# An FP4 feed-forward's weights: turned by TensorE from raw tiles, or loaded in 32 by 32 blocks and turned in place by VectorE

## The chip, the cores and the metric

The kernel runs on one core of a Trainium2 chip. The metric is the device time of one execution in microseconds (us), and the median of several runs is compared. A profile of one execution gives the time of every instruction on the engines: TensorE (PE, with its weight loads as PEld), VectorE (DVE), ScalarE (ACT), GpSimd (POOL) and SyncE (SP), whose queue issues nearly all DMA transfers.

## The reference, cut to what matters

One transformer layer in float32 over x of 8 sequences, 1,024 tokens, 512 features: a latent attention block with 16 heads (causal softmax, clipped scores, rotary part), then a feed-forward block whose matrices and activations are quantized to FP4 (E2M1) in blocks of 16 along the contracted dimension.

```
def fp4_quant_dequant(x):            # blocks of 16 along the last dim
    scale = max(max|x| of the block / 6, 1e-12)
    return nearest value of (0, .5, 1, 1.5, 2, 3, 4, 6) to |x / scale| * sign * scale

def fp4_linear(x, w):                # w is (n, k)
    return einsum('bsk,nk->bsn', fp4_quant_dequant(x), fp4_quant_dequant(w))

x = x + attention(layernorm(x))
x = x + fp4_linear(silu(fp4_linear(y, w_gate)) * fp4_linear(y, w_up), w_down)   # y = layernorm(x)
```

w_gate and w_up are 1408 by 512, w_down is 512 by 1408. They are quantized along their rows, but the matmuls contract over those rows' elements, so the kernel needs them turned: the contracted dimension on the partitions.

## The kernel before, in words

The work is cut into 16 units of 512 tokens (two per sequence). `attention(u)` runs over four groups of four heads, and in each over the key blocks: 3 score steps per group in the even units (12 in all), 7 in the odd ones (28), which also see the first half of their sequence. A score step (`score_step`) has TensorE write scores of four heads into the one PSUM score tile `sc_ps`; ScalarE takes the exponential into a tile `pT` (a ring of three, which the output projection's `wo` shares); the clamp that stands for the clip is done for one half by VectorE (L645) and for the other by GpSimd (L648); on the diagonal GpSimd masks (L653). TensorE then multiplies by the values (`num`), one score step late (`flush(1)`), so that the next scores stand ahead of it in its order. In even units VectorE sums the probabilities (L680), in the first odd ones TensorE does (`den`). At the end of a group VectorE turns and inverts the sums (L737 to L740).

Between score steps the function pops *fillers*: pieces of the next unit's projections (loading x, L375; norms; from unit 4 on, and for unit 2, VectorE turns x in blocks and 16 DMAs per 256 tokens, L410, move the blocks into `xnT`), and in units 0 to 3 the pieces of the weight preparation. From unit 4 on the fillers are the feed-forward of earlier units. The output projection of unit u-1 (`po`, four tiles, 14 us of TensorE) runs in unit u behind the DMA of `wo` (L795), with VectorE adding the residual (L814) and SP storing it (`mid`).

TensorE, VectorE, ScalarE and GpSimd execute in the order in which the program writes their instructions. The SP queue's order is chosen by the scheduler of the language, which puts transfers that wait for nothing early. SP keeps eight semaphores for its DMAs; a transfer waits for the one eight before it.

A small planner (`Clock`) keeps estimated times of the engines. VectorE work without a fixed place is put into two queues by `slack`, and laid into estimated gaps (`fill`). `need(key)` lays everything up to the last entry of that key at once.

The weights: `weight_pieces` cuts w_gate and w_up into 11 chunks of 128 rows, w_down into 4. `load(i)` fetches a chunk into raw tiles of 128 rows by up to 512 columns (L310, rows of 2 KB) and queues `quantize` on them: per part a block maximum (L226), six short scale instructions for the whole step (L242 to L247), then per part six passes (L266, L274, L277, twice L280, L262). A `piece` then needs that chunk, has TensorE turn it in 128 by 128 squares (`turn`, L208) into a PSUM bank of the shared ring of three, and ScalarE copies the bank into the final tile `wg_T`, `wu_T` or `wd_T` (L210). The same `quantize` serves the activations, which are kept turned already: there, with `turned=True`, VectorE's block transpose (L236) is laid before the maximum and after the last pass.

How many weight pieces each of the first four units takes is written out by hand:

```
if u < FIRST:
    upto = n_weights * (5, 16, 23, 37)[u] // 37
```

Of the kernel before, what the change touches and what calls it, by code (L numbers as in the profile page):

```python
# [11 lines left out]
F32 = mybir.dt.float32  # L12
# [6 lines left out]
P = 128  # L19
# [8 lines left out]
NDC = D // P  # L28
NFC = FF // P
BLK = 16  # L30
FCH = [(0, 512), (512, 512), (1024, 384)]
# [11 lines left out]
def tile_mla_then_fp4_ffn(  # L43
# [17 lines left out]
    nc = tc.nc  # L61
# [5 lines left out]
    ring = ctx.enter_context(tc.tile_pool(name="ring", bufs=9))  # L67
# [12 lines left out]
    class Clock:  # L80


        pe = dve = act = silu = 0.0
# [27 lines left out]
    clk = Clock()  # L111
# [91 lines left out]
    def turn(src, dst, n):  # L203

        pt = bank("pt").rearrange("p (n k) -> p n k", k=P)
        tile_shape("whole")
        for i in range(n):
            nc.tensor.transpose(pt[:, i, :], src[:, i * P : (i + 1) * P], ident)  # L208
            clk.pe += 0.11
        on_act(0.56, lambda: nc.scalar.copy(dst, pt[:, 0:n, :]))  # L210


    def quantize(parts, key, turned=False, ready=0.0):

        ends, at = [], 0
        for part in parts:
            ends.append((at, at + part.shape[1] // BLK))
            at = ends[-1][1]
        nb = at
        got = {}  # L220

        def amax(k):
            if k == 0:
                got["sc"] = p1.tile([P, 88], F32, tag="sc", name="sc")[:, :nb]
                got["rs"] = p1.tile([P, 88], F32, tag="rs", name="rs")[:, :nb]
            nc.vector.tensor_reduce(  # L226
                got["rs"][:, slice(*ends[k])],
                parts[k].rearrange("p (b k) -> p b k", k=BLK),
                AX.X,
                ALU.max,  # L230
                apply_absolute_value=True,
            )

        def turn_blocks(part):
            slack(
                0.06 + 0.0013 * part.shape[1], lambda: nc.vector.transpose(part, part), key  # L236
            )

        def scales():
            sc, rs = got["sc"], got["rs"]  # L240

            nc.vector.tensor_scalar(sc, rs, 1.0 / 6.0, None, ALU.mult)  # L242
            nc.vector.scalar_tensor_tensor(rs, sc, -4.0, rs, ALU.mult, ALU.add)
            nc.vector.scalar_tensor_tensor(rs, sc, -2.0, rs, ALU.mult, ALU.add)
            nc.vector.scalar_tensor_tensor(sc, rs, 1.0 / 6.0, sc, ALU.mult, ALU.add)
            nc.vector.tensor_scalar(sc, sc, 1e-12, None, ALU.max)
            nc.vector.reciprocal(rs, sc)  # L247

        for k, part in enumerate(parts):
            if turned:  # L250
                turn_blocks(part)
            slack(0.06 + 0.0012 * part.shape[1], lambda k=k: amax(k), key, ready=ready)
        slack(1.1 + 0.008 * nb, scales, key)
        for part, end in zip(parts, ends):
            step, bl = part.shape[1], slice(*end)
            nbl = step // BLK
            part3 = part.rearrange("p (b k) -> p b k", k=BLK)

            def times(which, part3=part3, bl=bl, nbl=nbl):
                by = got[which][:, bl].unsqueeze(2).to_broadcast([P, nbl, BLK])  # L260
                if which == "sc":
                    nc.vector.tensor_tensor(part3, part3, by, ALU.mult)  # L262
                else:


                    nc.vector.scalar_tensor_tensor(  # L266
                        part3, part3, BELOW_ONE, by, ALU.mult, ALU.mult
                    )

            def steps(part=part, step=step):
                got["m"] = m = p1.tile([P, 512], F32, tag="m", name="m")[:, :step]
                nc.vector.tensor_scalar(  # L274
                    m.bitcast(U32), part.bitcast(U32), EXP_MASK, None, ALU.bitwise_and
                )
                nc.vector.tensor_scalar(m, m, 1.0, MAGIC, ALU.max, ALU.mult)  # L277

            def to_grid(op, part=part):
                nc.vector.tensor_tensor(part, part, got["m"], op)  # L280

            pass_cost = 0.06 + 0.00125 * step
            slack(pass_cost, lambda f=times: f("rs"), key)
            slack(1.2 * pass_cost, steps, key)
            slack(pass_cost, lambda f=to_grid: f(ALU.add), key)
            slack(pass_cost, lambda f=to_grid: f(ALU.subtract), key)
            slack(pass_cost, lambda f=times: f("sc"), key)
            if turned:
                turn_blocks(part)


    def weight_pieces():

        chunks = []
        for c in range(NFC):
            rows = slice(c * P, (c + 1) * P)
            chunks.append([(w_gate[rows, :], wg_T[:, :, rows]), (w_up[rows, :], wu_T[:, :, rows])])
        for c in range(NDC):
            rows = slice(c * P, (c + 1) * P)
            chunks.append([(w_down[rows, :], wd_T[:, :, rows])])  # L300
        raws = {}

        def load(i):

            raws[i] = []
            for src, _ in chunks[i]:
                for off in range(0, src.shape[1], 512):
                    width = min(512, src.shape[1] - off)
                    raw = ring.tile([P, 512], F32, tag="h", name="wraw")[:, :width]
                    nc.sync.dma_start(out=raw, in_=src[:, off : off + width])  # L310
                    raws[i].append(raw)
            quantize(raws[i], ("w", i))

        def piece(i, k, dst, off, n):
            clk.need(("w", i))
            turn(raws[i][k], dst[:, off : off + n], n)
            if k == len(raws[i]) - 1:
                raws.pop(i)
                if i + 3 < len(chunks):
                    load(i + 3)  # L320

        pieces = []
        for i, parts in enumerate(chunks):
            if len(parts) > 1:
                pieces += [(i, k, dst, 0, NDC) for k, (_, dst) in enumerate(parts)]
            else:
                pieces += [
                    (i, k, parts[0][1], off // P, width // P) for k, (off, width) in enumerate(FCH)
                ]
        begun = [(0.5, lambda i=i: load(i)) for i in range(3)]  # L330
        return begun + [(0.5, lambda x=x: piece(*x)) for x in pieces]


    def normed(xt, key):
# [564 lines left out]
    def up(m, k):  # L899
        while silus:  # L900
            silus.popleft()()
        h = hs[m][k]
        pg = hidden(m, wu_T, k)
        on_dve(
            0.1 + 0.00115 * h.free_size(),
            max(clk.pe + 0.3, clk.silu),
            lambda: nc.vector.tensor_tensor(h, pg, h, ALU.mult),  # L907
        )
        for group in ((0, 1), (2, 3), (4,), (5,)) if m == pairs - 1 else ((0, 1), (2, 3), (4, 5)):
            if k == group[-1]:  # L910
                quantize([flat(hs[m][j]) for j in group], ("h", m, k // 2), True)
        if k == NS - 1:
            yTs.pop(m)

# [101 lines left out]
    for u in range(n_units):  # L1016
        if u > 0:
            urgent.extend(lambda t=t, aTs=aTs: out_proj(u - 1, t, aTs) for t in range(NT))
        own = []
        if u + 1 < n_units:  # L1020
            own.extend(project_pieces(u + 1))
            content, rotary = quad_pieces(u + 1, 0)
            own.extend([(1.7, content), (0.9, rotary)])
        take = []
        if u < FIRST:
            upto = n_weights * (5, 16, 23, 37)[u] // 37
            while weight_work and n_weights - len(weight_work) < upto:
                take.append(weight_work.popleft())

            for _ in range(8 if u == FIRST - 1 else 0):  # L1030
                c, n, run = ffn.popleft()
                take.append((c, run, n))
        else:

            left = sum((13, 5)[v % 2 == 0] for v in range(u, n_units))
            within = sum(c for c, n, _ in ffn if n < len(tiles) - NT)
            budget = within * (13, 5)[u % 2 == 0] / left
            if u in (n_units - 3, n_units - 2):

                budget -= 40.0  # L1040
            while ffn and budget > 0 and ffn[0][1] < NT * u:
                c, n, run = ffn.popleft()
                budget -= c
                take.append((c, run, n))
        fillers.extend(merged(own, take))
        aTs = attention(u)
        while fillers:
            fillers.popleft()[1]()
# [88 lines left out]
```

## Time and profile before

| what | value |
|---|---|
| median of 3 runs | 3523.83 us (3519.83 to 3523.85) |
| the profiled execution | 3518.86 us, its span 3517.1 us |
| PE, DVE, ACT, POOL busy in the span | 98%, 83%, 38%, 22% |
| first and last transposing matmul on a raw weight tile | 67.6 and 424.0 us |
| raw weight tiles: transposing matmuls, ScalarE copies, loads | 132, 34, 34 |
| DMA traffic of the execution | 148.46 MB, 190,066 packets |

A line of the page or of an answer names the source line, the engine, the operation, the tiles (output, then inputs) and the shape; "128x512 f32 x30 | 23.6, 786" are 30 instructions, busy 23.6 us in sum, 786 ns each in the mean; a third number is the time for which the engine stood idle ahead of them, and behind an arrow what ended that. In a view by windows each engine has its busy time and its count of instructions in the stretch. The timeline gives start, length, engine, line and tiles.

### The profile page before, as it was taken

To read this page: it belongs to the slowest core of one execution; us is meant where nothing else is said; L and a number is where in the kernel's file an instruction comes from. 1 tells how busy PE (TensorE), PEld (TensorE's weight loads), DVE (VectorE), ACT (ScalarE), POOL (GpSimd) and SP (SyncE) were. 2 spreads that over 40 slices of the span, in tenths; PEclk is the share of its full clock that TensorE was granted. 3 is DMA by queue.
4 is the path that set the end of the run, shared out by engine and by line. 5 is a ranking of instruction groups with operands and counts; after the bars stand their busy time and mean duration, and the time that the engine had idled before them with its cause. 6 is when DMAs were issued, how large, how long until landed. Compare 5 with 4: busy or idle time off the path is not lost. (4 is left out here: it accounts for less than half of the span.)

```text
span 3517.1 us, 101866 instructions
## 1 busy us (share of the span) xinstructions
PE 3440.5 (98%) x45428; PEld 1526.8 (43%) x45428; DVE 2923.4 (83%) x5308; ACT 1326.2 (38%) x1850; POOL 769.0 (22%) x1086
## 2 busy tenths in 40 slices
PE   8999999999999999999999999999999999999999
PEld 3333344444444444444444444444444444444444
DVE  6878759789977889887989778899778988699887
ACT  4444443434333343333343333434343333333211
POOL 3333322112121221221221212212212222111100
PEclk9999999999999999999999999999999999999999
DMA  3212111111021101121110211111211111100110
GB/s 98 70 49 71 47 36 52 50 36 30 20 64 32 55 26 32 35 59 50 32 32 20 67 29 54 30 32 32 61 49 32 32 32 49 50 20 20 56 32 17
DMA packets 190066, 148.46 MB, mean 42 GB/s; under 512 B 126524, under 2 KB 128060, under 8 KB 189628
## 3 DMA queue, kind: packets, MB, share of 16 engines
q1 hardware_dynamic: 187780, 141.09, 13.5%
q8 instruction: 356, 5.83, 0.7%
q10 hardware_dynamic: 1848, 0.87, 0.1%
q14 instruction: 82, 0.67, 0.1%
HBM read 94.72 MB, written 33.55 MB: 36 GB/s over the span
## 5 line engine op out<-in xcount | busy, mean ns | idle before, releaser
L629 ACT ACTIVATE pT<-sc_ps 128x1024 f32<-128x1024 f32 (+1 forms) x640 | 566.3, 937 | 1069.4 <-PE sc_ps L122 835.8
L648 POOL TENSOR_SCALAR pT<-pT 128x1024 f32<-128x1024 f32 (+1 forms) x320 | 337.7, 1055 | 2325.4 <-ACT pT L629 2247.0
L122 PE MATMUL pg<-yT,wu_T 128*32 128x256 f32 x11264 | 638.5, 380 | 0.0
L122 PE MATMUL pg<-yT,wg_T 128*32 128x256 f32 x11264 | 634.5, 379 | 1.7 <-ACT yT L859 0.8
L122 PE MATMUL pd<-wd_T,h 128*32 128x512 f32 x5632 | 616.8, 592 | 2.9 <-DVE h L236 2.9
L122 PEld LDWEIGHTS pg<-yT,wg_T 128*32 128x32 f32 x11264 | 366.2, 110 | 276.9 <-issue 37.2
L680 DVE TENSOR_TENSOR pT<-pT 128x1024 f32<-128x1024 f32 (+3 forms) x528 | 459.8, 898 | 25.3 <-POOL pT L653 21.7
L122 PEld LDWEIGHTS pg<-yT,wu_T 128*32 128x32 f32 x11264 | 360.0, 110 | 264.6 <-issue 33.5
L645 DVE TENSOR_SCALAR pT<-pT 128x1024 f32<-128x1024 f32 (+1 forms) x320 | 229.3, 716 | 195.8 <-ACT pT L629 194.7
L122 PEld LDWEIGHTS pd<-wd_T,h 128*32 128x32 f32 x5632 | 182.3, 110 | 415.8 <-issue 389.8
L122 PE MATMUL sc_ps<-qc,kT 32*128 32x512 f32 (+3 forms) x3072 | 338.3, 525 | 10.8 <-ACT pT L629 10.8
L141 ACT COPY h<-pg 128x512 f32<-128x512 f32 x192 | 105.5, 550 | 629.6 <-PE pg L122 629.6
L122 PE MATMUL num<-pT,v 128*32 128x512 f32 (+3 forms) x3072 | 314.0, 496 | 17.4 <-POOL pT L653 16.9
L122 PE MATMUL sc_ps<-qr,kr 32*128 32x512 f32 (+3 forms) x3072 | 306.3, 483 | 6.9 <-DVE qr L564 6.7
L280 DVE TENSOR_TENSOR h<-h,m 128x512 f32<-128x512 f32 (+1 forms) x384 | 259.6, 676 | 10.1
L236 DVE STREAM_TRANSPOSE h<-h 128x512 f32<-128x512 f32 (+1 forms) x384 | 249.9, 658 | 4.9
L653 POOL TENSOR_SCALAR_AFFINE_SELECT pT<-pT 128x256 f32<-128x256 f32 (+1 forms) x384 | 231.3, 622 | 25.2 <-DVE pT L645 10.7
L122 PE MATMUL po<-wo,aT 128*32 128x512 f32 x2048 | 225.1, 596 | 9.1 <-DMA wo<-in_w_o_dram 4.5
L907 DVE TENSOR_TENSOR h<-pg,h 128x512 f32<-128x512 f32 x192 | 122.9, 640 | 118.5 <-PE pg L122 110.6
L122 PEld LDWEIGHTS sc_ps<-qc,kT 32*128 32x128 f32 x3072 | 114.3, 183 | 208.7 <-issue 149.8
L122 PEld LDWEIGHTS sc_ps<-qr,kr 32*128 32x128 f32 x3072 | 144.0, 185 | 114.1 <-issue 77.8
L122 PEld LDWEIGHTS num<-pT,v 128*32 128x32 f32 x3072 | 64.5, 108 | 220.8 <-issue 119.0
(97 smaller groups left out, 3528.5 us busy)
## 6 DMA issues: line engine op xcount, KB each, us to landing
xo<-in_x_dram SPq DMA_DIRECT2D x64, 256.0 KB, 2.7
wo<-in_w_o_dram SPq DMA_DIRECT2D x16, 1024.0 KB, 5.2
mid<-xo SPq DMA_DIRECT2D x64, 256.0 KB, 2.8
y<-mid SPq DMA_DIRECT2D x64, 256.0 KB, 2.8
xr<-mid SPq DMA_DIRECT2D x64, 256.0 KB, 2.7
out_dram<-xr SPq DMA_DIRECT2D x64, 256.0 KB, 2.0
xp<-in_x_dram SPq DMA_DIRECT2D x30, 512.0 KB, 3.8
xnT<-xp SPq DMA_DIRECT2D x416, 32.0 KB, 2.0
```

Of the source, the lines that this page charges most:

```text
L122: nc.tensor.matmul(dst, **kw)
L141: on_act(0.1 + 0.0009 * src.free_size(), lambda: nc.scalar.copy(dst, src))
L236: 0.06 + 0.0013 * part.shape[1], lambda: nc.vector.transpose(part, part), key
L280: nc.vector.tensor_tensor(part, part, got["m"], op)
L629: lambda: nc.scalar.activation(part, sc[:, 2 * k : 2 * k + 2, :cols], AF.Exp, scale=SM_SCALE),
L645: lambda: nc.vector.tensor_scalar(part, part, E_HI, E_LO, ALU.min, ALU.max),
L648: nc.gpsimd.tensor_scalar(part, part, E_HI, E_LO, ALU.min, ALU.max)
L653: nc.gpsimd.affine_select(out=diag, in_=diag, pattern=[[0, 2], [0, len(segs)], [1, P]], compare_op=ALU.is_ge, fill=0.0, base=0, channel_mu ...
L680: lambda a=whole, b=part: nc.vector.tensor_tensor(a, a, b, ALU.add),
L907: lambda: nc.vector.tensor_tensor(h, pg, h, ALU.mult),
```

## The change

Weights are no longer loaded as rows into raw tiles. Each part of the final tile (128 partitions, up to 512 columns) is loaded by four DMAs, one for each 32 partitions; a DMA takes blocks of 32 rows by 32 columns (pieces of 128 B) to where the turned block will stand. `quantize` runs in place on two such parts at a time. Behind the last pass, VectorE's block transpose turns each 32 by 32 block where it lies. The matmuls on the identity and the ScalarE copies go. There are 9 works (three column ranges of each of gate and up, three groups of chunks of w_down), 35 parts, 18 quantizing steps and 140 DMAs; with the two first loads and a last `need`, 21 pieces, divided over the units as 4, 10, 16, 21. A work is loaded two works ahead, and a step needs the one before it to be laid.

```diff
-    def quantize(parts, key, turned=False, ready=0.0):
+    def quantize(parts, key, before=False, after=False, ready=0.0):
...
         for k, part in enumerate(parts):
-            if turned:
+            if before:
                 turn_blocks(part)
...
-            if turned:
+            if after:
                 turn_blocks(part)
...
-        chunks = []
-        for c in range(NFC):
-            rows = slice(c * P, (c + 1) * P)
-            chunks.append([(w_gate[rows, :], wg_T[:, :, rows]), (w_up[rows, :], wu_T[:, :, rows])])
-        for c in range(NDC):
-            rows = slice(c * P, (c + 1) * P)
-            chunks.append([(w_down[rows, :], wd_T[:, :, rows])])
-        raws = {}
+        works = []
+        for off, width in FCH:
+            for w, dst in ((w_gate, wg_T), (w_up, wu_T)):
+                src = w[off : off + width, :].rearrange("(f a) (c q b) -> q c a f b", a=32, q=4, b=32)
+                parts = [dst[:, c, off : off + width] for c in range(NDC)]
+                works.append((src, parts))
+        src = w_down.rearrange("(f a) (c q b) -> q c a f b", a=32, q=4, b=32)
+        for c0, n in ((0, 4), (4, 4), (8, 3)):
+            cs = range(c0, c0 + n)
+            works.append((src[:, c0 : c0 + n], [wd_T[:, c, :] for c in cs]))
 
         def load(i):
-            raws[i] = []
-            for src, _ in chunks[i]:
-                for off in range(0, src.shape[1], 512):
-                    width = min(512, src.shape[1] - off)
-                    raw = ring.tile([P, 512], F32, tag="h", name="wraw")[:, :width]
-                    nc.sync.dma_start(out=raw, in_=src[:, off : off + width])
-                    raws[i].append(raw)
-            quantize(raws[i], ("w", i))
-
-        def piece(i, k, dst, off, n):
-            clk.need(("w", i))
-            turn(raws[i][k], dst[:, off : off + n], n)
-            if k == len(raws[i]) - 1:
-                raws.pop(i)
-                if i + 3 < len(chunks):
-                    load(i + 3)
...
+            src, parts = works[i]
+            for k, part in enumerate(parts):
+                for q in range(4):
+                    nc.sync.dma_start(
+                        out=part[32 * q : 32 * q + 32, :].rearrange("a (f b) -> a f b", b=32),
+                        in_=src[q, k],
+                    )
+
+        def piece(i, k):
+            parts = works[i][1]
+            if k == 0 and i + 2 < len(works):
+                load(i + 2)
+            quantize(parts[k : k + 2], ("w", i, k), after=True)
+            before = (i, k - 2) if k else (i - 1, 2)
+            clk.need(("w", *before), pe=False)
+
+        steps = [(i, k) for i in range(len(works)) for k in (0, 2)]
+        begun = [(0.5, lambda i=i: load(i)) for i in range(2)]
+        last = lambda: clk.need(("w", *steps[-1]))
+        return begun + [(2.0, lambda x=x: piece(*x)) for x in steps] + [(0.5, last)]
...
-            upto = n_weights * (5, 16, 23, 37)[u] // 37
+            upto = n_weights * (4, 10, 16, 21)[u] // 21
```

More of the change, by code (lines that the diff above doesn't have):

```diff
@@ L322, in weight_pieces @@
[L322 to L331, printed above, removed]
+        works = []
@@ L910, in up @@
             if k == group[-1]:
-                quantize([flat(hs[m][j]) for j in group], ("h", m, k // 2), True)
+                quantize([flat(hs[m][j]) for j in group], ("h", m, k // 2), True, True)
         if k == NS - 1:
```

## The prediction

> **What bounds the kernel now.** I read the busy table first, then groups by shape, then busy time by stretch, then the engines' timelines at the places that the new instruction order changes.
>
> ```profile
> PE 3440.5 (98%) x45428; PEld 1526.8 (43%) x45428; DVE 2923.4 (83%) x5308; ACT 1326.2 (38%) x1850; POOL 769.0 (22%) x1086
> ```
>
> TensorE (PE) is the bound over the whole span, VectorE (DVE) second. But weights are prepared only in the first 430 us, and behind that the changed kernel's instruction order equals the old one on every engine. So the change is decided in the first four units (512 tokens each). The stretches below run from the first rotary multiply (L564) of one unit to that of the next; units 2 and 3 are cut at three clamps (L645: unit 2's fifth, unit 3's third and fourth). Columns: stretch, length, then PE, PEld, DVE, ACT, POOL busy, clock, DMA.
>
> ```profile
> 24.90:93.30 68.40, 61.05 (x712) 25.45 (x712) 59.68 (x100) 36.42 (x55) 35.11 (x48) 0.98 0.14 49
> 93.30:241.80 148.50, 142.09 (x1472) 53.64 (x1476) 120.34 (x211) 70.86 (x93) 48.30 (x62) 1.00 0.20 60
> 241.80:284.70 42.90, 38.34 (x399) 14.45 (x402) 27.57 (x52) 17.74 (x27) 12.88 (x21) 1.00 0.31 101
> 284.70:339.60 54.90, 53.47 (x632) 22.25 (x624) 51.11 (x87) 30.12 (x46) 28.43 (x38) 1.00 0.17 54
> 339.60:363.80 24.20, 20.03 (x168) 6.48 (x168) 23.24 (x45) 2.56 (x5) 1.84 (x2) 0.93 0.22 77
> 363.80:480.10 116.30, 111.84 (x1196) 43.93 (x1192) 76.20 (x135) 63.47 (x87) 44.05 (x61) 1.00 0.13 33
> ```
>
> The later part of unit 2 and its passage into unit 3 (284.7 to 363.8) already has DVE at 93 to 96%: no room for more there. Units 1 and 3 have 28 and 40 us of DVE idle.
>
> **Removed: TensorE transposes and ScalarE copies.**
>
> ```profile
> L208 PE MATMUL pt<-ident,wraw x132: 272/273/330, 67.6 to 424.1; 128*128 128x128 f32 x132
> L210 ACT COPY wg_T<-pt x11: 585/587/619, 68.3 to 328.8; 128x512 f32<-128x512 f32 x11
> ```
>
> The matmuls overlap: in the PE timeline a group of four holds PE 0.59 us, seven 0.91, eight 1.02. By unit 0 to 3 they are 8, 44, 28 and 52 matmuls, or 1.1 + 6.2 + 3.9 + 6.9 = 18.0 us. Not all of it is on the path:
>
> ```profile
> 149.14 1.14 PE L122 MATMUL sc_ps<-qc,kT 32*128 32x512 f32 x8 [0.26 <-ACT pT L629]
> 153.25 1.14 PE L122 MATMUL sc_ps<-qc,kT 32*128 32x512 f32 x8 [0.26 <-ACT pT L629]
> 157.04 1.09 PE L208 MATMUL pt<-ident,wraw 128*128 128x128 f32 x8
> 158.06 1.14 PE L122 MATMUL sc_ps<-qc,kT 32*128 32x512 f32 x8
> ```
>
> Without a transpose, a score step takes 4.11 us and ends on the exponential (one score tile in PSUM); with eight it takes 4.81. So a group of eight is worth 0.70, not 1.02, and one of four (122.82 to 127.19, 4.37) 0.26, not 0.59. I credit 2 us to unit 1 and 3.5 to unit 3 behind 363.8. The 34 ScalarE copies (20 us) are credited nothing: ACT is under 56% busy in every stretch, which hides them. The PSUM bank that each group took, and SP's waits for a free raw tile, cost the path nothing now: loads had landed long before their first pass.
>
> **Added: VectorE transposes, and other places for the passes.** Column counts are unchanged (16,896). Rows, 0 to 480 us (count | busy, mean):
>
> ```profile
> L280 DVE TENSOR_TENSOR wraw<-wraw,m 128x512 f32<-128x512 f32 x60 | 45.7, 761 | 1.6
> L262 DVE TENSOR_TENSOR wraw<-wraw,sc 128x512 f32<-128x512 f32 x30 | 23.6, 786 | 0.8
> L266 DVE SCALAR_TENSOR_TENSOR wraw<-wraw,rs 128x512 f32<-128x512 f32 x30 | 23.4, 779 | 0.4
> L737 DVE STREAM_TRANSPOSE rc<-den 128x512 f32<-128x512 f32 x15 | 10.6, 706 | 2.0 <-PE den L122 2.0
> ```
>
> The 35 transposes are 33 of 512 columns in all, at 0.70 us: 23 us. There are 18 scale steps for 15, at 1.6: 5 us more. What matters is where they stand. Counting each DVE instruction of both orders at the median of its line and width: unit 0 falls from 56.8 to 48.6 us, unit 1 rises from 113.5 to 119.3, **unit 2 from 63.3 to 91.7, against its length of 82.8**, unit 3 from 110.4 to 111.5. The shares 4, 10, 16, 21 of 21 give unit 2 (12 score steps) six quantizing steps, as many as unit 1 (28 score steps), and each `need` of an older step lays it out at once.
>
> The window 284.7 to 339.6 by hand. Before, its groups sum to 56.2 us: 18.8 for weights, 37.4 for attention (51.1 as they overlap, so attention 32.3). After, the same ten score steps hold five weight steps. A 512-column part costs 0.69 + 0.43 + 0.43 + 2x0.69 + 0.69 + 0.70 = 4.3, a 384-column part 3.4 by its own rows: 4x4.3 + 6x3.4 = 37.8; maxima 4x0.68 + 4x0.54 = 4.9; scales 7.6. Sum 50.3. Attention keeps 33.3 of its 37.4, 28.8 as they overlap. 79.1 + 3 of idle = 82 for 54.9: **+27**. Bounds: +24 with no idle, +33 if the passes run at the means above (761 to 786) and not at the medians near 0.69. A clamp has about 2.4 us before its weighing matmul misses it, so PE waits for nearly all of it: ten score steps cannot be overtaken, with one score tile and three pT buffers. PE waits then follow the clamps; where PE waited 3.1 us for L814 (339.6 to 363.8) the mean clock was 0.93, and I leave 2 us for that inside the bounds.
>
> Behind it, four output-projection tiles: DVE count 18.4 for 24.6; PE needs 3 (to the last L740), 13.9, then 3.2 to the next clamp: 20 for 24.2: **-4**. Unit 0: VectorE is 8 us lighter and PE waited 1.7 and 1.6 for L564 behind it: -3.
>
> **Moved: 140 loads for 34 on SP's queue.** They need nothing, so they stand early: 48 ahead of unit 1's second x pair (L375, issued at 48.98), 101 ahead of the first `wo` (103.2), all 140 ahead of the first xnT turn (150.6). A load is 512 pieces of 128 B; no row has it. The nearest:
>
> ```profile
> 7.49 3.17 SPq L195 DMA_DIRECT2D wqc<-in_w_q_dram  x1
> 10.71 2.80 SPq L196 DMA_DIRECT2D wqr<-in_w_q_dram  x1
> L410 SPq DMA_DIRECT2D xnT<-xp x416: 585/610/2157, 150.6 to 2960.3; - x139
> L310 SPq DMA_DIRECT2D wraw<-in_w_gate_dram x11: 328/333/677, 15.5 to 222.0; - x11
> ```
>
> Those of L195 and L196 are 2,048 such pieces from HBM, 0.70 to 0.79 us per 512. xnT is 256 pieces, 0.61 (0.65 apart); a straight line through 128 pieces (0.33) and 256 gives 1.17. I take 0.70, since L196 has piece size and source. SP's loads begin at 15.5 and the first x pair (1.34 us) stands among them; so the second leaves at 17 + 48x0.70 = 51, lands 3.8 later (row of xp) at 54 to 55, and VectorE wants it at 53.4, with everything queued behind it: the clamp, the sums. I charge +3 (0 to 4), which cancels unit 0's gain. `wo` is behind unit 2's first x pair (free to go at 71.2, when its buffer is read) and 37 loads: 71.2 + 1 + 37x0.70 = 98 < 103.2; xnT waits for the last 25 loads behind unit 0's stores (about 124): 124 + 18 = 142 < 150.6. The mid stores and xo loads between them wait at most 9 loads, 6 us, and their readers come later. At 1.17 the first costs 24 and `wo` 12 more.
>
> The Trainium skill, page "DMA: Bandwidth & Descriptors", section "Rules for kernel authors", speaks against this load: under 64 KB a transfer is mostly overhead; its fit of 2.0 us plus bytes over 436 GB/s would make 2.15 each, and if they went one by one the x pair would leave at 120 and the kernel lose some 65 us (an estimate from that page). The xnT rows say that 2.0 us is the landing time, while the next leaves 0.65 later, so I don't follow it.
>
> The page "VectorE: DVE Perf Modes", "Rules for kernel authors", sends a 128x128 turn to TensorE where PSUM will do, and gives 311 ns for VectorE's (bf16); four of them, 1.24 us per part, would add some 5 us to the window. The 0.70 row decides.
>
> **Sum.** 0 (unit 0) - 2 + 27 - 4 - 3.5 = +17.5 on the profiled 3518.86: 3536. That execution lies 5 below the median of the runs (3523.83) and 1 below their lowest; at the runs' level I say 3540. About 0.2% (7 us) is what a measurement of this kernel can tell from no change.
>
> **Rivals.** (a) Forecast, unit 2 bound by VectorE: 3532 to 3552, chance 0.61. (b) Loads late: from a spacing of 0.9 on, VectorE waits for the x pair and PE for `wo`; at 1.17, +36 on top, 3576. For it: rows 32 apart in HBM, 64 KB steps; against: L196. Chance 0.19. (c) Faster: clamps in unit 2 aren't held up, because VectorE finishes each weight step before the next exponential ends. Then -3 - 2 - 4 - 3.5 = -12 remains, 3511. It decides at a lag of 2.4 us per clamp; against it stand three intervals between clamps of 12 to 15 us of DVE work where 4 to 7 elapsed. Chance 0.09. (d) Half the excess is taken up by TensorE running ahead: about 3527, 0.11.
>
> The range 3526 to 3572 takes in (a), most of (d), and (b) short of its end. Faster 0.09, same 0.10, slower 0.81.
>
> **What would show it.** The window from unit 2's fifth clamp to unit 3's third should be about 82 us with DVE over 93% and PE under 70% busy; weight loads 0.65 to 0.8 apart; the second x pair issued near 51; PE waits named L645 or POOL behind it. Wrong if PE stays over 90% there, if the loss sits before 120 us, or if loads still run at 150 us.

## The result and the profile after

The changed kernel takes 3554.74 us (median of 4 runs, 3553.56 to 3556.05) where the kernel before takes 3523.3; the ratio is 1.0091, 95% interval 1.0074 to 1.0109. It is slower, by about twice what was forecast, and inside the range. The profiled execution took 3556.05 us, 37.2 above the profiled one of before, which happened to lie 4 us under its median.

The busy table of the changed kernel: TensorE lost 132 matmuls but only 1.3 us (in the fourth stretch below 644 matmuls took 64.9 us at a clock of 0.81, where 632 had taken 53.5 at 1.00), VectorE gained 60 instructions and 28 us.

```profile
PE 3439.2 (97%) x45296; PEld 1515.8 (43%) x45296; DVE 2951.2 (83%) x5368; ACT 1308.4 (37%) x1816; POOL 764.8 (22%) x1086
```

The same six stretches as before, cut at the same instructions (stretch, length, then PE, PEld, DVE, ACT, POOL busy, clock, DMA):

```profile
24.90:91.00 66.10, 59.17 (x701) 24.90 (x704) 51.91 (x83) 35.05 (x53) 34.30 (x48) 0.97 0.60 109
91.00:240.00 149.00, 138.32 (x1440) 48.21 (x1432) 124.18 (x217) 64.70 (x82) 49.38 (x64) 1.00 0.28 60
240.00:282.20 42.20, 36.88 (x372) 13.53 (x376) 28.80 (x54) 15.61 (x24) 12.35 (x20) 0.96 0.25 86
282.20:377.90 95.70, 64.85 (x644) 24.76 (x632) 85.22 (x158) 28.68 (x42) 24.02 (x33) 0.81 0.06 19
377.90:398.40 20.50, 16.56 (x132) 4.51 (x136) 17.40 (x36) 1.10 (x2) 2.67 (x6) 0.80 0.27 90
398.40:516.90 118.50, 108.44 (x1156) 39.98 (x1152) 78.50 (x138) 57.93 (x76) 43.92 (x61) 0.99 0.10 24
```

The loss is in the fourth line; the others add up to 4 us less than before. From unit 2's fifth clamp to unit 3's third, 54.9 us have become 95.7, with VectorE 89% busy, TensorE 68%. Four long waits of TensorE end there (engine, tile, line, waited for: total, times, longest), all ended by something that stood in VectorE's queue or behind it:

```profile
PE den L122 <- DVE qr L558: 8.1, 1, 8.1
PE sc_ps L122 <- DVE qr L558: 6.9, 1, 6.9
PE num L122 <- POOL pT L647: 5.6, 1, 5.6
PE den L122 <- DVE pT L674: 4.7, 1, 4.7
```

The longest wait, 8.6 us, begins there at 373.3 and ends in the stretch behind it, when VectorE has divided by the sums (L734):

```profile
381.84 13.41 PE L122 MATMUL po<-wo,aT 128*32 128x512 f32 x104 [8.58 <-DVE aT L734]
```

L558, L647 and L674 are the rotary multiply, the diagonal mask and the sums (L564, L653, L680 before; from about L326 on the changed file's numbers are 6 smaller). Removed work: the transposes and their copies that are left are those of x alone (duration min/median/max, first and last start; eight more matmuls, on x in a tile named `y`, stand at 15.9).

```profile
L208 PE MATMUL pt<-ident,xp x40: 272/273/478, 6.3 to 307.7; 128*128 128x128 f32 x40
...
L210 ACT COPY xnT<-pt x12: 583/586/618, 7.5 to 315.8; 128x512 f32<-128x512 f32 x12
```

Added work: the turns, and the passes now on the final tiles, VectorE's groups by shape over 0 to 520 us.

```profile
L280 DVE TENSOR_TENSOR wd_T<-wd_T,m 128x512 f32<-128x512 f32 x22 | 17.4, 790 | 0.7
L262 DVE TENSOR_TENSOR wd_T<-wd_T,sc 128x512 f32<-128x512 f32 x11 | 9.6, 876 | 0.4
L236 DVE STREAM_TRANSPOSE wd_T<-wd_T 128x512 f32<-128x512 f32 x11 | 7.8, 705 | 0.2
L266 DVE SCALAR_TENSOR_TENSOR wd_T<-wd_T,rs 128x512 f32<-128x512 f32 x11 | 7.4, 674 | 0.2
```

A turn of 512 columns takes 0.705 us; the row of the division (L737) had said 0.706. The loads in SP's timeline (start, duration of the group):

```profile
17.28 11.15 SPq L309 DMA_DIRECT2D wg_T<-in_w_gate_dram  x15
28.47 8.90 SPq L309 DMA_DIRECT2D wu_T<-in_w_up_dram  x16
37.42 9.78 SPq L309 DMA_DIRECT2D wg_T<-in_w_gate_dram  x16
49.22 0.39 SPq L369 DMA_DIRECT2D xp<-in_x_dram  x1
```

By the mean of each group they leave 0.56 to 0.74 us apart, and the second x pair (L369, L375 before) leaves at 49.22, where it left at 48.98.

### The profile page after: what moved, and what is told of

The parts are those of the page before. It is cut to its first block, busy times and chain, and to the rows that moved or that the text cites. A ratio compares the mean times of both kernels' runs of the same rounds, so it can differ in the third digit from the quotient of the medians.

```text
span 3554.3 us, 101732 instructions
## 1 busy us (share of the span) xinstructions
PE 3439.2 (97%) x45296; PEld 1515.8 (43%) x45296; DVE 2951.2 (83%) x5368; ACT 1308.4 (37%) x1816; POOL 764.8 (22%) x1086
## 5 line engine op out<-in xcount | busy, mean ns | idle before, releaser
L674 DVE TENSOR_TENSOR pT<-pT 128x1024 f32<-128x1024 f32 (+3 forms) x528 | 461.2, 901 | 22.2 <-POOL pT L647 18.4
L280 DVE TENSOR_TENSOR h<-h,m 128x512 f32<-128x512 f32 (+1 forms) x384 | 259.5, 676 | 10.1
L236 DVE STREAM_TRANSPOSE h<-h 128x512 f32<-128x512 f32 (+1 forms) x384 | 249.8, 658 | 4.9
L647 POOL TENSOR_SCALAR_AFFINE_SELECT pT<-pT 128x256 f32<-128x256 f32 (+1 forms) x384 | 231.0, 621 | 42.1 <-DVE pT L639 28.0
```

Source lines behind the costliest of these rows:

```text
L647: nc.gpsimd.affine_select(out=diag, in_=diag, pattern=[[0, 2], [0, len(segs)], [1, P]], compare_op=ALU.is_ge, fill=0.0, base=0, channel_mu ...
L674: lambda a=whole, b=part: nc.vector.tensor_tensor(a, a, b, ALU.add),
```

## The experiments

Two measures serve throughout. The **shift** is how much later than in the kernel before a clamp runs in the profiled execution; from unit 4's first clamp to the end it changes by less than 1.5 us. The **counted lateness** is worked out from the instruction order alone: VectorE's instructions between two clamps, each at its median in the trace of before (a turn at 0.70), less the interval between the same clamps in that trace; what exceeds 2.4 us of play is summed. Lateness that a clamp passes on is not counted twice. The count first stands on record behind the results of the runs on placement, crowding, loads and missing turns; ahead of their results it stands for three: turns in the kernel before, an older step laid out later, and both edits.

**Placement.** The changed kernel with other shares:

```diff
-            upto = n_weights * (4, 10, 16, 21)[u] // 21
+            upto = n_weights * (4, 11, 13, 21)[u] // 21
```

> The changed kernel with other shares: (4, 11, 13, 21) of 21 instead of (4, 10, 16, 21), so four quantizing steps leave unit 2, one for unit 1 and three for unit 3. Loads, block transposes and all else stay. VectorE's counted work in units 0 to 3 becomes 48.6, 132.1, 58.0, 131.0 us (changed kernel: 48.6, 119.3, 91.7, 111.5; lengths before 68.4, 148.5, 82.8, 155.5). Theory (the loss is placement, unit 2 overfilled): the clock time from unit 2's fifth clamp to unit 3's third falls from 95.7 to 53 to 58 us, TensorE is over 90% busy in it, and the kernel takes 3515 to 3532 us, within 8 of the kernel before; clamps in unit 3 may fall a few us late. Rival (the new loads or the block transposes cost the time wherever they stand): 3545 to 3560.

Measured: 3542.4 us, 1.0060 (1.0047 to 1.0072), between the two theories. The window did what the theory says, but time went somewhere else. Its windows are the slow stretch, the out-projection, and clamps 12 to 22 of unit 3:

```profile
284.80:337.40 52.60, 49.81 (x612) 20.89 (x608) 45.01 (x77) 27.27 (x42) 24.04 (x32) 1.00 0.10 31
337.40:355.80 18.40, 17.81 (x164) 5.20 (x160) 12.88 (x29) 3.66 (x5) 3.18 (x7) 1.00 0.31 112
394.30:467.40 73.10, 55.23 (x564) 20.49 (x556) 56.27 (x102) 24.00 (x33) 19.99 (x28) 0.86 0.10 24
```

At unit 3's twelfth clamp this kernel is 9.0 us ahead of the one before. It loses 27.7 in the last of these lines, where VectorE is only 77% busy and idle for 16.8 us. The same ten intervals between clamps before:

```profile
403.30:448.70 45.40, 42.64 (x494) 17.39 (x494) 16.35 (x29) 23.07 (x32) 17.46 (x29) 1.00 0.14 36
```

VectorE's 56.3 us of work alone are 10.9 more than their 45.4; the other 16.8 us of the loss are as much as its idle time. TensorE waits there four times for clamped or masked scores, 17.0 us in all:

```profile
PE num L122 <- POOL pT L647: 10.9, 3, 6.3
PE num L122 <- DVE pT L639: 6.1, 1, 6.1
```

So a unit need not be full to be late (131.0 us were counted for unit 3, of 155.5): it is enough that a few of its intervals are. A new step lays out at once all that is left of the step before it, and the instruction counts of single intervals show the lumps: about 11, 9 and 12 us of VectorE work between two clamps that stood 3.0 to 4.7 us apart. A clamp behind such a lump is late, and VectorE has nothing to do afterwards until TensorE and ScalarE have produced the next scores.

**The old kernel, crowded.** The kernel before with its own loads and TensorE's transposes:

```diff
-            upto = n_weights * (5, 16, 23, 37)[u] // 37
+            upto = n_weights * (5, 13, 26, 37)[u] // 37
```

> The kernel before, with its own loads and TensorE's transposes, and only the shares changed from (5, 16, 23, 37) to (5, 13, 26, 37) of 37: three pieces move from unit 1 and three from unit 3 into unit 2. VectorE's counted work in units 0 to 3 becomes 56.8, 101.9, 87.5, 97.9 us (from 56.8, 113.5, 63.3, 110.4), so unit 2 has more VectorE work than its length of 82.8. Theory (placement alone makes the loss): slower than before by 10 to 30 us, 3533 to 3553, with VectorE the bound of a stretch in unit 2. Rival (it takes the new loads or block transposes): within 5 us of the kernel before.

Measured: 3540.72, 1.0056 (1.0042 to 1.0070): 19 us lost with no new load and no new turn. The stretch from unit 2's fifth clamp to unit 3's third, 54.9 us before:

```profile
284.00:363.70 79.70, 59.10 (x644) 25.25 (x640) 74.72 (x132) 32.25 (x50) 29.72 (x38) 0.89 0.16 47
```

VectorE is 94% busy. Placement alone makes such a loss.

**Loads.** The changed kernel with whole rows (`raw_rows`) in one DMA for each part:

```diff
+        def raw_rows(i, k, width):
...
-                for q in range(4):
-                    nc.sync.dma_start(
-                        out=part[32 * q : 32 * q + 32, :].rearrange("a (f b) -> a f b", b=32),
-                        in_=src[q, k],
-                    )
+                nc.sync.dma_start(out=part, in_=raw_rows(i, k, part.shape[1]))
```

> The changed kernel with each weight part loaded by one DMA of 128 whole rows (up to 2 KB each) instead of four DMAs of 512 pieces of 128 B; the block arrangement is left out, so the weights are wrongly arranged. 35 loads for 140. Theory (loads are hidden): within 3 us of the changed kernel, 3552 to 3558. Rival (loads late, or their traffic slows the engines in the window): 10 us or more below, under 3545.

Measured: 3555.24 (1.0098, 1.0084 to 1.0112), the changed kernel's time. The 140 loads of small pieces cost nothing that can be measured.

**The turns themselves.** The changed kernel without VectorE's turns of the weights:

```diff
-            quantize(parts[k : k + 2], ("w", i, k), after=True)
+            quantize(parts[k : k + 2], ("w", i, k))
```

> The changed kernel without VectorE's block transposes of the weights; the turn inside each 32 by 32 block is left out, so the weights are wrongly arranged. Loads, scales, passes and shares stay. Theory (placement): VectorE loses 22 us of work over units 0 to 3, but only ten transposes, 6 to 7 us, lie in the slow window, so the window falls from 95.7 to about 82 to 90 and the kernel from 3554.7 to 3540 to 3548: 7 to 15 of the 31 us come back. Rival (the transposes themselves are the loss): all comes back, 3518 to 3530.

Measured: 3545.45, 1.0073 (1.0061 to 1.0086): 9 us come back, not 31. In the slow window VectorE's busy time falls by 6.1 us (85.22 to 79.10) and the window by 6.5 (95.70 to 89.20): there VectorE's work sets the pace, one for one.

```profile
279.70:368.90 89.20, 63.49 (x644) 23.86 (x632) 79.10 (x148) 28.70 (x42) 23.44 (x33) 0.84 0.06 20
```

The same 23 us of turns in the kernel before, on the raw pieces (which leaves the weights wrongly arranged):

```diff
-            if turned:
+            if turned or key[0] == "w":
                 turn_blocks(part)
```

> The kernel before plus VectorE's block transposes of every raw weight piece after its quantizing, about 23 us more VectorE work, in the old loads, shares and TensorE transposes; the weights are wrongly arranged. Between no two clamps does the counted VectorE work then exceed the interval by more than 0.2 us beyond the 2.4 us of play. Theory (the work costs little where it is spread): 0 to 6 us slower than the kernel before, 3522 to 3528. Rival (block transposes cost their own time): 23 us slower, 3545.

Measured: 3528.66, 1.0022 (1.0013 to 1.0032): 7 us slower, a third of the work, just above the expected range. Counted lateness says 0.2 and misses this: the shift grows by 1 to 5 us at a time, in units 1 to 3, where it sees less than the play. What makes it grow there stays open.

**The removed TensorE work.** The kernel before without its transposes of weights:

```diff
-            turn(raws[i][k], dst[:, off : off + n], n)
+            raw = raws[i][k]
+            on_act(
+                0.56,
+                lambda: nc.scalar.copy(
+                    dst[:, off : off + n], raw.rearrange("p (n k) -> p n k", k=P)
+                ),
+            )
```

> The kernel before without TensorE's transposes of the weights: ScalarE copies each raw piece straight into the final tile, so the turn is left out and the weights are wrongly arranged. TensorE loses 132 matmuls, 18.0 us of its time; VectorE's work and its order stay. Theory (part of that time is beside the path): 5.5 to 8 us faster than the kernel before, 3514 to 3518 against 3521.6. Rival (all of it is on the path): 18 us faster, 3504.

Measured: 3515.96, 0.9987 (0.9979 to 0.9996): 5.3 us faster, of 18.0 us of TensorE time. The theory holds: over two thirds of it lay beside the path. That it lay beside ScalarE's exponentials is read from the 4.11 us steps alone.

**The lumps.** The changed kernel with its own shares, and the older step laid out one step later:

```diff
-            before = (i, k - 2) if k else (i - 1, 2)
-            clk.need(("w", *before), pe=False)
+            clk.need(("w", i - 1, k), pe=False)
```

> The changed kernel with its own shares (4, 10, 16, 21), and only the second edit: each new step lays out at once what is left of the step two before it, not of the one just before. Counted lateness falls from 28.0 to 16.9 us (12.2 in unit 2, 4.7 in unit 3). Theory: the measured shift is 1.3 times the counted one, so 22 us where it was 37, and the kernel takes 3536 to 3544. Rival (only the shares matter): 3550 or more.

Measured: 3537.97, 1.0050 (1.0038 to 1.0063). Half the loss goes, with the same shares: a step's remainder is laid out later, in smaller lumps, and part of it behind the slow stretch:

```profile
278.10:360.20 82.10, 59.67 (x644) 23.29 (x632) 74.17 (x137) 28.39 (x42) 23.74 (x33) 0.90 0.07 22
```

The stretch is 13.6 us shorter, and 11.0 of these are VectorE work that now stands elsewhere. So this run does not tell what smaller lumps alone are worth.

**Both edits.** This order with shares (4, 12, 15, 21):

> The changed kernel with two edits in the order alone: shares (4, 12, 15, 21) of 21, and each new quantizing step lays out at once what is left of the step two before it, no longer of the step just before it. Counted lateness (VectorE's work between two clamps, each instruction at its median, above the interval between the same clamps in the kernel before, with 2.4 us of play, summed) is 28.0 us in the changed kernel, 17.8 in the one with shares (4, 11, 13, 21), 16.1 in the old kernel with crowded shares (measured shifts 37, 22, 20), and 1.3 here. Theory: the loss goes and the removed TensorE work shows, 3508 to 3522. Rival (the new kernel has another cost that placement does not reach): 3530 or more.

Measured: 3510.84 (7 runs), 0.9972 (0.9961 to 0.9983): 10 us faster than the kernel before, where the changed one is 31 slower, with the same loads and turns. The slow stretch and the out-projection:

```profile
279.40:336.40 57.00, 50.70 (x620) 20.78 (x608) 53.03 (x95) 28.30 (x42) 23.57 (x32) 1.00 0.09 31
336.40:354.00 17.60, 17.03 (x156) 5.20 (x160) 16.60 (x32) 1.04 (x2) 3.34 (x7) 1.00 0.32 106
```

The shifts beside the count (the runs with whole rows and, below, with matmuls by zeros keep the changed kernel's shift, +36.6 and +36.2):

| kernel | counted lateness, us | shift at unit 4, us | time, us |
|---|---|---|---|
| changed | 28.0 | +36.9 | 3554.74 |
| changed, no turns | 22.4 | +28.7 | 3545.45 |
| changed, shares (4, 11, 13, 21) | 17.8 | +22.0 | 3542.4 |
| changed, older step laid out later | 16.9 | +18.0 | 3537.97 |
| before, crowded | 16.1 | +19.2 | 3540.72 |
| changed, both edits | 1.3 | -9.2 | 3510.84 |
| before, no TensorE transposes | 0 | -5.1 | 3515.96 |
| before, turns added | 0.2 | +12.5 | 3528.66 |

Where the count is large, the shift is 1.1 to 1.3 times it.

**The half clock.** In the slow window TensorE ran at a mean clock of 0.81. Behind the wait of 8.1 us eight matmuls took nearly twice the 1.04 us that eight of this shape took in unit 1:

```profile
316.02 1.93 PE L122 MATMUL den<-pT,ones 128*32 128x512 f32 x8 [8.06 <-DVE qr L558]
```

The Trainium skill, page "TensorE: Matmul & The Clock Gate", section "Why this matters for your kernels", warns of idle gaps over some 3 us between bursts of matmuls, behind which the clock falls to half; this row agrees. To see if that is part of the loss, matmuls by zeros fill the waits (the sums are unchanged; the same fill stands ahead of `den` and of the second half of the scores):

```diff
+    WARM = {("num", 2, 1, 2): 4, ("den", 2, 1): 6, ("den", 2, 2): 3, ("sc", 3, 0, 0): 5}
...
             clk.pe = max(clk.pe, ready)
+            warm("num", u, hq, j)
```

> The changed kernel with matmuls by a tile of zeros (they add nothing) placed on TensorE just ahead of the four long waits of the slow window (5.6 us before num, 8.1 and 4.7 before den, 6.9 before the second half of the scores): 4, 6, 3 and 5 groups of four, about 1 us each, so that what is left of each wait is under 2.5 us. The order on the other engines is that of the changed kernel. In the changed kernel TensorE's clock was 0.81 in the window and VectorE idle for 10.5 of its 95.7 us. Theory (the half clock behind each wait makes the next clamp late and is the mis-sized part of the window): the clock in the window rises to 0.95 or more, VectorE's idle time falls to 4 to 6 us, the window to 88 to 92, and the kernel to 3547 to 3552. Rival (VectorE's own work sets the window, the clock only fills the waits): the clock rises but the window stays at 95 to 97 and the time within 2 us of 3554.

Measured: 3554.69, 1.0099 (1.0082 to 1.0116), the changed kernel's time. The window:

```profile
282.50:377.20 94.70, 76.08 (x786) 28.85 (x776) 85.33 (x158) 28.46 (x42) 23.50 (x33) 0.92 0.06 19
```

The clock rose to 0.92, not to the 0.95 wanted, since two waits stayed at 4.7 and 3.0 us; VectorE's busy time is the same to 0.1 us, and the window 1.0 shorter. The rival is right in the time, and the theory's 88 to 92 us for the window is refuted: as far as the fill reached, the half clock fills waits and costs about a microsecond there. What is left of it was not tried, nor was the longest wait, ahead of the out-projection, where TensorE has the work: the 104 matmuls behind it took 13.41 us, and in the kernel with both edits 128 of them took 13.94 without such a wait. By that rate the half clock costs some 2 us there (an estimate); the kernel before pays 1.5, where the first 64 took 7.07 and the last 64, behind a wait of 3.1 us, 8.55.

## Why the prediction was right, and where its sum was off

The direction, the mechanism and the place were right; the main term was too small, and two small ones had the wrong sign. That the range held is partly luck: 3554.74 lies above the 3532 to 3552 that forecast (a) gave itself, and inside the whole range only because that was stretched for late loads, which did not come. By the shift of the clamps:

| step | forecast, us | measured, us |
|---|---|---|
| unit 0 | 0 | -2.4 |
| unit 1 | -2 | +1.8 |
| unit 2 up to its fifth clamp | none | -1.9 |
| window to unit 3's third clamp | +27 | +40.8 |
| out-projection | -4 | -3.8 |
| unit 3's rest | -3.5 | +2.4 |
| sum | +17.5 | +36.9 |

- **The window, 82 us forecast, 95.7 measured**, is the mis-sized term, outside its own bounds of +24 to +33. Half of the missing 13.7 us is VectorE's busy time, 85.2 for 79.1. Passes and maxima of the same ten parts summed to 46.7 us where 42.7 were reckoned from medians: a 512-column L280 took 857 ns there on the mean, where 0.69 us was reckoned, so the means were the better price.

```profile
L280 DVE TENSOR_TENSOR wd_T<-wd_T,m 128x512 f32<-128x512 f32 x8 | 6.9, 857 | 0.3
```

 Six of these eight took 0.69 us; the other two, 1.20 and 1.51, had GpSimd at work beside them for 1.12 and 0.97. From 0 to 520 us all eight such passes of over 0.8 us (0.89 to 1.58) stand beside GpSimd's clamp or mask, as 14 of the 50 shorter ones do in part; no run tested whether that is the cause. The five scale groups took 9.4 for 7.6. The other half is idle time, 10.5 for 3. The forecast treated the window as an average, with VectorE never short of work. VectorE's own waits there say otherwise (after a lump it waits for the next exponential or sum; the rest of the 10.5 us is in gaps too short for this view):

```profile
DVE pT L639 <- ACT pT L623: 4.8, 6, 2.4
DVE rc L731 <- PE den L122: 2.0, 1, 2.0
DVE qr L558 <- PE pqr L122: 0.4, 1, 0.4
```

 That lumps cost time even in a unit that has room for its VectorE work is what unit 3 of the run with shares (4, 11, 13, 21) shows. How the 7.5 us divide among the lumps of this window was not measured; the clock was tried as their cause and accounts for about 1.
- **The signs.** TensorE's share of the window (68% busy), the loads and the x pair came as said. VectorE's share did not (89%, where over 93% was said), and no long wait of TensorE was for VectorE's clamp: one was for GpSimd's mask, the others for the rotary multiply, the sums and the division, which stand in the same queue.
- **Unit 1 and unit 3's rest.** Both were credited with the removed transposes, and both lost. In unit 1's score steps, 4.11 us long without a transpose before, TensorE now waits for the clamp and not for the exponential, and a step takes 4.55 to 5.02:

```profile
150.89 1.06 PE L122 MATMUL num<-pT,v 128*32 128x512 f32 x8 [0.87 <-DVE pT L639]
...
155.44 1.06 PE L122 MATMUL num<-pT,v 128*32 128x512 f32 x8 [0.70 <-DVE pT L639]
...
160.46 1.07 PE L122 MATMUL num<-pT,v 128*32 128x512 f32 x8 [1.17 <-DVE pT L639]
```

 "28 us of idle" in unit 1 was true for the sum and not for these steps. In unit 3's rest TensorE's waits for the clamp and the rotary multiply rose from 0.6 to 5.6 us. The credit itself, 5.5 us in all, was right only in its sum (5.3 alone), by luck: most of it lay in units 0 and 2; behind unit 3's fourth clamp the run without transposes gains nothing.
- **Loads.** The spacing, the x pair's issue and `wo` came as forecast (0.70, 51 and 98 there; 0.56 to 0.74, 49.22 and 100.80 here). The +3 for a late x pair did not come: unit 0 gained 2.4. Rival (b) falls, in the trace and in the run with whole rows. The fit that the prediction set against the loads, 2.0 us plus bytes over 436 GB/s, stands on its page in another section and for DMAs that GpSimd issues; SP issued these, and they landed after 2.1 to 2.6 us (medians by tile and size) while the next had left.
- **Rivals (c) and (d).** In this order they are refuted. But (c)'s sum, 12 us faster if no clamp is held up, is near what the kernel with both edits shows: 10 us. Its terms are not: by the shifts there, unit 0 gave 3.5 us and the out-projection 6.6, where 3 and 4 stood, but unit 1 lost 1.6 and unit 3's rest 0.6, where gains of 2 and 3.5 stood.

## What to carry to other kernels

Work that is moved to an engine with idle time must fit between the due times of what stands behind it there, not only into its share of a stage: count the work between neighbouring due points, at means, and compare it with their distance and the play. A scheduler that catches up on a backlog at once makes lumps that cost more than the busy share shows: they hold up the engine that waits for them, and leave their own engine idle afterwards. Before such a change is given up, move its work: here the same loads and turns gave 31 us more or 10 us less than before by two edits in the order.

## What was not expected of the hardware

- Waits of TensorE of 4.7 to 8.6 us go with half clock in the records behind them: the eight matmuls of `den` took 1.93 us after the wait of 8.1, where others of that shape took 1.04 in unit 1. As the fill showed, this costs little where another engine sets the pace.
- 140 DMAs of 384 or 512 pieces of 128 bytes, issued 0.56 to 0.74 us apart in unit 0 on one queue beside running compute (DMA share 0.60 over unit 0, 0.14 before), gave the same time as 35 of whole rows (3554.74 and 3555.24 us).
- A turn of 128x512 float32 took 0.70 to 0.71 us whether it read PSUM (L731) or turned an SBUF tile in place (L236). Yet 23 us of turns, spread over an order with no lump in it, cost 7 us.
